# Six products in stage 1, one operand by an adding DMA, and VectorE's steps in another order

## The chip, the cores and the metric

The kernel runs on one core of a Trainium2 chip, in float32. The metric is the device time of one execution in microseconds, from the program's first to its last instruction with what lies around it; the time before is the median of three runs. The engines are TensorE (PE, with its weight loads as PEld), VectorE (DVE), ScalarE (ACT), GpSimd (POOL) and SyncE (SP), which here only issues DMAs.

## The reference

For each of 128 samples, `x` (64 channels, 1024 positions) goes through four convolutions whose weights are scaled by the sample's own style vector and normalised; the sum with `x` is the result.

```python
def _layer(x, style, w, b, mw, mb, typ):
    s = style @ mw.T + mb
    weight = SCALE * w * s[:, None, :, None]
    demod = lax.rsqrt(jnp.sum(weight * weight, axis=(2, 3)) + EPS)
    weight = weight * demod[:, :, None, None]
    if typ == 'same':
        out = jax.vmap(_conv_same)(x, weight) + b[None, :, None]
    elif typ == 'upsample':
        out = jax.vmap(_conv_up)(x, weight.transpose(0, 2, 1, 3)) + b[None, :, None]
        out = _blur(out, 2.0 * blur_k, (1, 1))
    elif typ == 'downsample':
        xb = _blur(x, blur_k, (2, 2))
        out = jax.vmap(_conv_down)(xb, weight) + b[None, :, None]
    return out
...
out = x
for i, typ in enumerate(('same', 'upsample', 'same', 'downsample')):
    out = _layer(out, style, weights[i], biases[i], mod_w[i], mod_b[i], typ)
return x + out
```

## The kernel before, in words

Nothing nonlinear lies between the four layers, so the kernel multiplies their kernels together, sample by sample, into one convolution of nine taps, and applies that to `x` once. The first and last three positions of each row are computed apart ("ends", the border work), in small pieces that are strewn over the turns.

Samples are handled in fours ("quads" q = 0 to 31), two in the upper and two in the lower 64 partitions; every matmul uses a 64 by 64 quarter of the array, four quarters side by side. A quad goes through these steps:

- Stage 1 multiplies layer 4's three scaled taps (`wd`, made by `scale3`) with layer 3's three taps into five taps `S`. It does not do the nine tap products: `w3x` and `w2n` also hold sums of neighbouring taps. `stage1_a` (line 461) runs five blocks of 64 columns, ScalarE copies four of them into `S` with a minus, and `stage1_b` (line 473) runs two blocks more; then two VectorE instructions (line 481, the "S step") make the last two taps out of PSUM and `S`, and GpSimd adds two slots (line 484).
- Stage 2 (`stage2`) multiplies `S` with the blurred taps `E` of layer 2 into seven taps `R`. Turns 5 to 27 do part of it a turn ahead: `share_sums` (line 499, VectorE), `share` (TensorE) and `share_copy` (ScalarE, line 529), which lays the shared part into the PSUM banks `psR` of the same pool that `psS` of stage 1 held. So the share copy waits for the S step, and the next turn's stage 2 waits for the share copy. Where a turn's stage 2 isn't shared, it writes those banks itself and waits for the S step directly.
- Stage 3 (`stage3_b`, `stage3_a`) makes the nine taps `Wf`, with GpSimd's `r_sums` (line 638) ahead of its last product; VectorE combines them into `H` (`combine_a`, `combine_b`).
- The convolution: `x` lies in three planes by position modulo 3. VectorE forms `G` in two steps, G2 (`in_g2`, one plane, line 712) and G01 (`in_g01`, two planes, line 712); out of `G` come T0 and T4 (`in04`, VectorE, line 790), T1 (`in1`) and T2 (`in2`, both GpSimd, lines 776 and 781); out of `x` comes T3 (`in3`, VectorE, line 761). Five products on TensorE, `conv0` to `conv4` (line 803), use T0 to T4; `sum1`, `sum2` and ScalarE's output copies (line 880) end it.

The main loop, `turn_of(q)`, works on four quads at once: outputs and products of q, products of n = q + 1, stages 2 and 3 and inputs of c = q + 2, stage 1 of s = q + 4. Each engine takes its instructions in the order in which this code is written. Turn 4 is the "entry" turn, with an order of its own; turns 0 to 3 are `early_turn`. A turn begins with `stage2(c)` on TensorE. One piece of side work stands in most turns on VectorE (table `SIDE`): turns 5 to 7 read small products out of the upper columns of the PSUM tile `Y` (`small_rest`) and turns 4 to 6 clear those columns (MEMSET, line 1524); turns 8 to 28 do border work. A VectorE access of `Y` waits until ScalarE has copied turn q's output plane out of it. Turns 10, 14, 15 and 19 also run border matmuls on TensorE just ahead of conv1.

Of the kernel before, what the change touches and what calls it, by code (L numbers as in the profile page):

```python
# [54 lines left out]
C = 64  # L55
K = 3
# [7 lines left out]
def kernel(  # L64
# [30 lines left out]
    gpool = ctx.enter_context(tc.tile_pool(name="gpool", bufs=1))  # L95
# [308 lines left out]
    w3x = const.tile([P, 5, C], F32, name="w3x")  # L404
    w2n = const.tile([P, 5, C], F32, name="w2n")
# [9 lines left out]
    def scale3(q, engs=(nc_a, nc_a)):  # L415
# [3 lines left out]
        for j in range(2):  # L419
            t = wd_pool.tile([P, 5, C], F32, tag="wd", name=f"wd{q}_{j}")  # L420
# [23 lines left out]
    EVEN = slice(0, K, 2)  # L444

    def stage1(q, pool=None, engs=(nc_a, nc_a), between=None):
# [3 lines left out]
        for k, (at, at1) in enumerate(((0, 3), (3, 1), (1, 4))):  # L450
            tap_matmul(ps, wd, at, 2, woi[2][:, k, :], EVEN, first=k == 0)
            tap_matmul(ps, wd, at1, 1, woi[2][:, k, :], slice(1, 2), last=k == K - 1)
# [3 lines left out]
        for r in range(2):  # L456
            scaled_copy(engs[r], flat(st[r][:, 1:6]), ps[r][:, : 5 * C], tB[:, q, r : r + 1])
# [3 lines left out]
    def stage1_a(q, ps=None):  # L461
# [3 lines left out]
        tap_matmul(ps, wd, 2, 2, w2n[:, 0, :], EVEN, first=True)  # L465
        tap_matmul(ps, wd, 3, 2, w2n[:, 2, :], EVEN)
        tap_matmul(ps, wd, 1, 1, w2n[:, 1, :], slice(1, 2))
        st, t = s_tiles(q)
        for r in range(2):
            scaled_copy(nc_a, flat(st[r][:, :4]), ps[r][:, C : 5 * C], tBn[:, q, r : r + 1])  # L470
        chain[q] = wd, ps, st, t

    def stage1_b(q):

        wd, ps, st, t = chain[q]
        tap_matmul(ps, wd, 2, 1, w2n[:, 3, :], slice(3, 4))
        tap_matmul(ps, wd, 4, 1, w2n[:, 4, :], slice(4, 5), last=True)
        for r in range(2):
            p1 = st[r][:, 0:1, :].to_broadcast([P, 2, C])
            sums = ps[r][:, 2 * C : 6 * C].rearrange("c (a b o) -> c a b o", a=2, b=2)[:, :, 0]  # L480
            nc_v.scalar_tensor_tensor(
                st[r][:, 4:6, :], sums, tB[:, q, r : r + 1], p1, op0=ALU.mult, op1=ALU.subtract
            )
        nc_g.tensor_add(t[:, :, 2], t[:, :, 2], t[:, :, 0])  # L484
# [14 lines left out]
    def share_sums(q):  # L499
        t = whole[q]  # L500
        nc_v.tensor_add(t[:, :, 6:8], t[:, :, 1:5:3], t[:, :, 2:6:3])
# [13 lines left out]
    def share(q, ps):  # L515
# [3 lines left out]
        chain_matmul(p12, E[:, 2], chain[q], slice(6, 7))  # L519
        chain_matmul(p34, E[:, 6], chain[q], slice(6, 7))  # L520
        chain_matmul(p34, E[:, 5], chain[q], slice(7, 8), True)
# [13 lines left out]
    def stage2_rest(q):  # L535
# [17 lines left out]
            (block(4), Ed[:, 5], slice(4, 5)),
            (block(5), E[:, 7], slice(5, 6)),
# [222 lines left out]

    def in2(q, eng):
# [13 lines left out]
    def product(q, m, ps, groups=range(K), alone=False):  # L792

        W, H_ = Wq[q]
        tag, i = SLOT[m]
        for g in groups:
            for s, rows in enumerate(HALF):
                for c, cols in enumerate(HALF):
                    if m in (0, 4):
                        w = W[rows, tap(m // 2, g), c, :]  # L800
                    else:
# [4 lines left out]
                        Ts[q, tag][rows, c, i, g : g + NB],  # L806
# [83 lines left out]

    raw = const.tile([P, 512], F32, name="raw")
# [97 lines left out]
    g1 = const.tile([P, 6, C], F32, name="g1")  # L989
# [732 lines left out]
```

## Time and profile before

| | |
|---|---|
| Runs | 474.98, 476.53 and 475.28 us; median 475.28 |
| Profiled execution, first to last instruction | 475.5 us (what lies around it is not shown) |
| TensorE busy, share of the span | 469.7 us, 99% |
| VectorE busy | 417.3 us, 88% |
| ScalarE busy | 312.0 us, 66% |
| GpSimd busy | 165.8 us, 35% |
| Mean granted TensorE clock | 0.998 |
| One turn without border matmuls (6 to 27) | 13.8 to 14.2 us |
| One turn with them | 15.5 to 16.6 us |
| Data moved by DMA | 70.71 MB, 149 GB/s |

A line of the timeline reads: start in us from the span's start, duration, engine, line of the kernel, operation, output <- inputs, shape, count. Where several instructions are drawn together, the duration is that of all of them. Matmuls are pipelined, so the start of the next group tells more than a group's end; a float32 matmul is two instructions. In the view of one line's instructions the three numbers are the shortest, median and longest duration in ns; in the list of DMA issues they are count, size and median time to landing.

### The profile page before, as it was taken

To read this page: it belongs to the slowest core of one execution; us is meant where nothing else is said; L and a number is where in the kernel's file an instruction comes from. 1 tells how busy PE (TensorE), PEld (TensorE's weight loads), DVE (VectorE), ACT (ScalarE), POOL (GpSimd) and SP (SyncE) were. 2 spreads that over 40 slices of the span, in tenths; PEclk is the share of its full clock that TensorE was granted. 3 is DMA by queue.
4 is the path that set the end of the run, shared out by engine and by line. 5 is a ranking of instruction groups with operands and counts; after the bars stand their busy time and mean duration, and the time that the engine had idled before them with its cause. 6 is when DMAs were issued, how large, how long until landed. Compare 5 with 4: busy or idle time off the path is not lost.

```text
span 475.5 us, 26771 instructions
## 1 busy us (share of the span) xinstructions
PE 469.7 (99%) x11932; PEld 349.5 (74%) x11932; DVE 417.3 (88%) x694; ACT 312.0 (66%) x711; POOL 165.8 (35%) x200
## 2 busy tenths in 40 slices
PE   9999999999999999999999999999999999999996
PEld 6987788777678876677776677766788787876653
DVE  3889998879989998899979899979998999999896
ACT  4565657577766676766667666667666777766464
POOL 3634033664444342233432233422333423243200
PEclk9999999999999999999999999999999999999999
DMA  5237456535445554345544454543555544455225
GB/s 176 71 115 224 150 151 180 152 113 177 139 145 166 166 166 136 123 150 169 163 150 126 130 168 152 178 124 121 152 164 169 164 145 147 148 152 161 80 91 193
DMA packets 52707, 70.71 MB, mean 149 GB/s; under 512 B 6000, under 2 KB 50672, under 8 KB 52592
## 3 DMA queue, kind: packets, MB, share of 16 engines
q1 hardware_dynamic: 52368, 68.78, 46.3%
q8 instruction: 93, 1.52, 1.4%
q10 hardware_dynamic: 224, 0.22, 0.1%
q14 instruction: 22, 0.18, 0.1%
HBM read 35.36 MB, written 33.62 MB: 145 GB/s over the span
## 4 chain that ended last, share of the span: by engine, by line
PE 99%; DVE 0%; ACT 0%; issue 0%
PE psA L803 47%; PE Y L803 12%; PE psR L506 9%; PE psW L621 7%; PE psA L621 7%; PE psS L428 6%; PE psR L589 5%; PE psA L506 2%; PE Y L1044 2%; PE Y L183 1%; PE Y L379 1%; PE psM L220 0%; PE psE L1044 0%; PE Y L255 0%; DVE o L882 0%; PE psM L255 0%
## 5 line engine op out<-in xcount | busy, mean ns | idle before, releaser
L803 PE MATMUL psA<-T,H 64*64 64x340 f32 x2304 | 185.9, 446 | 0.0
L803 PEld LDWEIGHTS psA<-T,H 64*64 64x64 f32 x2304 | 90.7, 133 | 46.9 <-issue 2.5
L712 DVE SCALAR_TENSOR_TENSOR G<-X 128x1376 f32<-128x1376 f32 (+2 forms) x65 | 78.0, 1206 | 0.2
L776 POOL TENSOR_TENSOR T<-G 128x684 f32<-128x684 f32 x28 | 46.3, 1652 | 73.7 <-DVE G L712 73.7
L484 POOL TENSOR_TENSOR S<-S 128x128 f32<-128x128 f32 x28 | 21.6, 772 | 139.7 <-ACT S L399 139.6
L399 ACT ACTIVATE R<-psR,tC 128x448 f32<-128x448 f32 x63 | 36.6, 631 | 43.6 <-PE psR L506 25.8
L803 PE MATMUL psA<-T,Wf 64*64 64x340 f32 x768 | 63.7, 446 | 0.0
L803 PE MATMUL Y<-T,Wf 64*64 64x340 f32 x768 | 62.4, 451 | 0.0
L712 DVE SCALAR_TENSOR_TENSOR Y<-m,psA 128x340 f32<-128x340 f32 x62 | 32.0, 516 | 28.2 <-PE psA L803 26.9
L399 ACT ACTIVATE psW<-psA 128x128 f32<-128x128 f32 x100 | 19.3, 268 | 49.1 <-PE psA L621 45.0
L790 DVE TENSOR_TENSOR T<-G 128x1368 f32<-128x1368 f32 (+1 forms) x33 | 50.8, 1541 | 0.0
L399 ACT ACTIVATE Wf<-psW,t 128x256 f32<-128x256 f32 (+2 forms) x76 | 32.7, 480 | 26.7 <-PE psW L621 26.4
L761 DVE TENSOR_TENSOR T<-X 128x684 f32<-128x684 f32 x32 | 47.7, 1492 | 0.0
L506 PE MATMUL psR<-S,E 64*64 64x64 f32 (+1 forms) x1472 | 46.8, 237 | 0.0
L781 POOL TENSOR_TENSOR T<-G 128x684 f32<-128x684 f32 x28 | 46.5, 1660 | 0.0
L428 PEld LDWEIGHTS psS<-wd,w2n 64*64 64x64 f32 x1120 | 35.1, 133 | 12.9 <-issue 0.3
L506 PEld LDWEIGHTS psR<-S,E 64*64 64x64 f32 x1472 | 39.5, 134 | 4.9 <-ACT psR L529 0.2
L803 PEld LDWEIGHTS Y<-T,Wf 64*64 64x64 f32 x768 | 30.3, 132 | 16.8
L803 PEld LDWEIGHTS psA<-T,Wf 64*64 64x64 f32 x768 | 29.8, 133 | 14.5
L880 ACT ACTIVATE o<-psA,tb,td 128x340 f32<-128x340 f32 x63 | 37.1, 648 | 5.0 <-PE psA L803 2.8
L880 ACT ACTIVATE o<-y,tb,td 128x340 f32<-128x340 f32 x62 | 38.5, 678 | 0.0
L880 ACT ACTIVATE o<-Y,tb,td 128x340 f32<-128x340 f32 x62 | 36.1, 639 | 2.8 <-PE Y L803 2.0
(180 smaller groups left out, 840.4 us busy)
## 6 DMA issues: line engine op xcount, KB each, us to landing
out<-o SPq DMA_DIRECT2D x191, 170.0 KB, 2.6
X<-in_x SPq DMA_DIRECT2D x150, 172.0 KB, 3.4
X<-in_x SPq DMA_DIRECT2D x14, 516.0 KB, 5.0
par<-in_params SPq DMA_DIRECT2D x3, 192.0 KB, 3.8
Xe<-in_x_ends SPq DMA_DIRECT2D x1, 512.0 KB, 4.5
out<-Oe SPq DMA_DIRECT2D x2, 96.0 KB, 2.1
out<-o ACTq DMA_DIRECT2D x1, 170.0 KB, 2.8
par<-in_params SPq DMA_DIRECT2D x1, 160.0 KB, 2.7
```

Source lines behind the costliest of these rows:

```text
L399: nc_a.activation(dst, src, AF.Copy, scale=f)
L428: nc.tensor.matmul(ps[r][cols, at * C : (at + n) * C], weight[rows], wd[c if r == 0 else 1 - c][rows, taps], start=first, stop=last, skip_ ...
L506: nc.tensor.matmul(dst[r][cols], weight[rows], st[c if r == 0 else 1 - c][rows, slots, :], start=False, stop=last, skip_group_check=True,)
L589: nc.tensor.matmul(ps[r][cols, lo * C : (lo + m) * C], E[rows, e + 2, :], src[rows, a, :], start=(n == 0), stop=(n == 8), skip_group_check ...
L621: nc.tensor.matmul(dst[r][cols], weight[rows], t[rows, c, slots, :], start=first, stop=last, skip_group_check=True,)
L712: nc_v.scalar_tensor_tensor(out, x, f, y, op0=ALU.mult, op1=op)
L761: nc_v.tensor_sub(t[:, pairs, 0, :NJ], plane(X, 3, pairs), plane(X, 1, pairs))
L776: eng.tensor_add(t[:, :, 0, :NJ], plane(g, 2), plane(g, 1))
L781: eng.tensor_sub(t[:, :, 1, :NJ], plane(g, 2), plane(g, 1))
L790: nc_v.tensor_sub(t[:, pairs, :, :NJ], both(a, PL), both(b, 1))
L803: nc.tensor.matmul(ps[s][cols, :NB], w, Ts[q, tag][rows, c, i, g : g + NB], start=(g == 0 and (m == 3 or alone)), stop=(g == K - 1), skip_ ...
L880: nc_a.activation(dst, src, AF.Identity, bias=add, scale=d3)
```

## The change

1. `stage1_a` and `stage1_b` make the five taps from six products of one block (64 columns) each: the three products of equal taps, and three of sums of two taps. `w3x`, `w2n` and `wd` get a sixth block, 0 + 2. `stage1_a` runs the three of equal taps with a minus, ScalarE writes them in four copies (two end taps, and the middle one twice), and GpSimd makes with an add and a subtract the slot that the middle tap needs. `stage1_b` runs the other three, and the S step has 192 columns for 128. The whole form, `stage1` (quads 0, 1, 2 and 6), keeps its nine blocks in three instructions for six. The order of the slots in `S` changes everywhere with it.
2. From the entry turn on, T1 is no longer a GpSimd add into a tile: a DMA issued from GpSimd behind `r_sums` adds one plane of `G` onto another in place, and conv1 reads `G` (25 DMAs). T2 is then made a turn earlier, before that DMA. `G` gets a second buffer; `g1` and `raw` move into other tensors' space.
3. On VectorE the side work stands ahead of G2, G01 directly behind G2 and so ahead of the S step, and T0/T4 of c stands behind `sum1`, ahead of T3, where in the turn after it stood T0/T4 of n. The second half of the `g1` step moves from behind T3 in turn 13 to turn 14's side work.

```diff
-    gpool = ctx.enter_context(tc.tile_pool(name="gpool", bufs=1))
+    gpool = ctx.enter_context(tc.tile_pool(name="gpool", bufs=2))
...
         for t, src in ((w3x, w3), (w2n, woi[2])):
-            nc_g.tensor_add(t[:, K:], src[:, : K - 1], src[:, 1:])
+            nc_g.tensor_add(t[:, K : K + 2], src[:, : K - 1], src[:, 1:])
+            nc_g.tensor_add(t[:, K + 2], src[:, 0], src[:, 2])
...
     def stage1_a(q, ps=None):
...
-        tap_matmul(ps, wd, 2, 2, w2n[:, 0, :], EVEN, first=True)
-        tap_matmul(ps, wd, 3, 2, w2n[:, 2, :], EVEN)
-        tap_matmul(ps, wd, 1, 1, w2n[:, 1, :], slice(1, 2))
+        for n, (i, at) in enumerate(((0, 1), (2, 3), (1, 4))):
+            tap_matmul(ps, wd, at, 1, w2n[:, i, :], slice(i, i + 1), first=n == 0)
         st, t = s_tiles(q)
         for r in range(2):
-            scaled_copy(nc_a, flat(st[r][:, :4]), ps[r][:, C : 5 * C], tBn[:, q, r : r + 1])
+            ends = ps[r][:, C : 5 * C].rearrange("c (a b o) -> c a b o", a=2, b=2)[:, :, 0]
+            scaled_copy(nc_a, st[r][:, 0:5:4, :], ends, tBn[:, q, r : r + 1])
+        for r in range(2):
+            middle = ps[r][:, None, 4 * C : 5 * C].to_broadcast([P, 2, C])
+            scaled_copy(nc_a, st[r][:, 5:8:2, :], middle, tBn[:, q, r : r + 1])
+        nc_g.tensor_add(t[:, :, 6], t[:, :, 0], t[:, :, 4])
+        nc_g.tensor_sub(t[:, :, 6], t[:, :, 6], t[:, :, 5])
...
     def stage1_b(q):
-        tap_matmul(ps, wd, 2, 1, w2n[:, 3, :], slice(3, 4))
-        tap_matmul(ps, wd, 4, 1, w2n[:, 4, :], slice(4, 5), last=True)
+        for n, (i, at) in enumerate(((3, 1), (4, 3), (5, 2))):
+            tap_matmul(ps, wd, at, 1, w2n[:, i, :], slice(i, i + 1), last=n == K - 1)
         for r in range(2):
-            p1 = st[r][:, 0:1, :].to_broadcast([P, 2, C])
-            sums = ps[r][:, 2 * C : 6 * C].rearrange("c (a b o) -> c a b o", a=2, b=2)[:, :, 0]
             nc_v.scalar_tensor_tensor(
-                st[r][:, 4:6, :], sums, tB[:, q, r : r + 1], p1, op0=ALU.mult, op1=ALU.subtract
+                flat(st[r][:, 1:4]),
+                ps[r][:, C : 4 * C],
+                tB[:, q, r : r + 1],
+                flat(st[r][:, 5:8]),
+                op0=ALU.mult,
+                op1=ALU.subtract,
             )
-        nc_g.tensor_add(t[:, :, 2], t[:, :, 2], t[:, :, 0])
...
+    def in1_dma(q):
+
+        g = Gs[q]
+        nc_g.dma_start(plane(g, 2), plane(g, 1), accum_op=ALU.add)
+        first_of[q] = g[:, :, :PL]
...
+        14: lambda: setup1(1),
...
-    LATE = {13: lambda: setup1(1)}
...
     def turn_of(q):
...
             r_sums(c, nc_g)
+            in1_dma(n)
             sum2(q)
-            in2(n, nc_g)
...
-        in04(n)
+        if entry:
+            in04(n)
         if sharing(q):
             share_sums(c + 1)
-        in_g2(c)
         side(SIDE, q)
         if q in SMALL:
             l, bs = SMALL[q]
             nc_v.memset(high(bs.stop - bs.start), 0.0)
+        in_g2(c)
+        in_g01(c)
         conv0(q, *((2,) if entry else range(K)))
...
         if s < NQ:
             stage1_b(s)
-        in_g01(c)
...
+        in2(c, nc_g)
         sum1(n)
+        in04(c)
         in3(c)
-        side(LATE, q)
-        if s == NQ:
-            in04(c)
-        in1(c, nc_g)
```

How VectorE's rows stand in the entry turn: before (the MEMSET clears Y's upper columns, L481 is the S step, L712 on G are G2 and G01).

```order
L790 TENSOR_TENSOR T_5_1826<-G_1507 128x4x342
L712 SCALAR_TENSOR_TENSOR G_1828<-X_105 128x2x342
L279 TENSOR_TENSOR nw<-dm,var 128x96
L280 SCALAR_TENSOR_TENSOR nw<-nw,dm 128x96
L281 SCALAR_TENSOR_TENSOR dm<-nw,dm 128x96
L1524 MEMSET Y 128x96
L481 SCALAR_TENSOR_TENSOR S_1818<-psS_0_1804,tB,S_1818 128x128
L481 SCALAR_TENSOR_TENSOR S_1818<-psS_1_1805,tB,S_1818 128x128
L712 SCALAR_TENSOR_TENSOR G_1828<-X_105 128x2x688
L712 SCALAR_TENSOR_TENSOR y_5_1872<-psA_1722,m_5_1802 128x680
L761 TENSOR_TENSOR T_6_1874<-X_105 128x2x342
```

In the changed kernel VectorE's rows of the same turn are these.

```order
L803 TENSOR_TENSOR T_5_1810<-G_1492 128x4x342
L279 TENSOR_TENSOR nw<-dm,var 128x96
L280 SCALAR_TENSOR_TENSOR nw<-nw,dm 128x96
L281 SCALAR_TENSOR_TENSOR dm<-nw,dm 128x96
L1539 MEMSET Y 128x96
L717 SCALAR_TENSOR_TENSOR G_1816<-X_105 128x2x342
L717 SCALAR_TENSOR_TENSOR G_1816<-X_105 128x2x688
L482 SCALAR_TENSOR_TENSOR S_1798<-psS_0_1784,tB,S_1798 128x192
L482 SCALAR_TENSOR_TENSOR S_1798<-psS_1_1785,tB,S_1798 128x192
L717 SCALAR_TENSOR_TENSOR y_5_1861<-psA_1702,m_5_1782 128x680
L803 TENSOR_TENSOR T_6_1863<-G_1816 128x4x342
L766 TENSOR_TENSOR T_6_1865<-X_105 128x2x342
```

G2 has moved from ahead of the MEMSET to behind it, G01 from behind the S step to ahead of it, and a second T0/T4 row has come in ahead of T3.

VectorE in turn 5, the first of the three whose side work reads Y (the rows on `cc`); before, from T0/T4 to T3:

```order
L790 TENSOR_TENSOR T_6_2062<-G_1828 128x4x342
L501 TENSOR_TENSOR S_1818<-S_1818 128x2x128
L712 SCALAR_TENSOR_TENSOR G_2065<-X_106 128x2x342
L980 TENSOR_TENSOR cc_149<-Y,a_142 128x96
L981 SCALAR_TENSOR_TENSOR cc_149<-b1s,cc_149 128x96
L1524 MEMSET Y 128x96
L481 SCALAR_TENSOR_TENSOR S_2057<-psS_0_2043,tB,S_2057 128x128
L481 SCALAR_TENSOR_TENSOR S_2057<-psS_1_2044,tB,S_2057 128x128
L712 SCALAR_TENSOR_TENSOR G_2065<-X_106 128x2x688
L712 SCALAR_TENSOR_TENSOR y_6_2132<-psA_1950,m_6_2060 128x680
L761 TENSOR_TENSOR T_7_2134<-X_106 128x2x342
```

VectorE in turn 5 of the changed kernel:

```order
L506 TENSOR_TENSOR S_1798<-S_1798 128x2x128
L995 TENSOR_TENSOR cc_148<-Y,a_141 128x96
L996 SCALAR_TENSOR_TENSOR cc_148<-b1s,cc_148 128x96
L1539 MEMSET Y 128x96
L717 SCALAR_TENSOR_TENSOR G_2059<-X_106 128x2x342
L717 SCALAR_TENSOR_TENSOR G_2059<-X_106 128x2x688
L482 SCALAR_TENSOR_TENSOR S_2046<-psS_0_2032,tB,S_2046 128x192
L482 SCALAR_TENSOR_TENSOR S_2046<-psS_1_2033,tB,S_2046 128x192
L717 SCALAR_TENSOR_TENSOR y_6_2128<-psA_1939,m_6_2053 128x680
L803 TENSOR_TENSOR T_7_2130<-G_2059 128x4x342
L766 TENSOR_TENSOR T_7_2132<-X_106 128x2x342
```

Ahead of the side work's read of Y only the share sums (on S) are left of what stood there; both G steps now stand between the side work and the S step, and T0/T4 between `sum1` (on y) and T3. The later turns are built the same way, with their own side work.

GpSimd in turn 12, from its R sums on (the row on S is the add of stage 1, the rows on T are T2 and T1); before:

```order
L638 TENSOR_TENSOR R_3858<-R_3858 128x2x128
L781 TENSOR_TENSOR T_13_3796<-G_3729 128x2x342
L484 TENSOR_TENSOR S_3991<-S_3991 128x2x64
L776 TENSOR_TENSOR T_14_4066<-G_3999 128x2x342
L638 TENSOR_TENSOR R_4128<-R_4128 128x2x128
```

GpSimd in turn 12 of the changed kernel:

```order
L643 TENSOR_TENSOR R_3896<-R_3896 128x2x128
L786 DMA G_3763<-G_3763 128x2x342
L472 TENSOR_TENSOR S_4029<-S_4029 128x2x64
L473 TENSOR_TENSOR S_4029<-S_4029 128x2x64
L794 TENSOR_TENSOR T_14_4105<-G_4040 128x2x342
```

The DMA stands where T2 stood, T2 (of the next quad) where T1 stood, and the one row on S has become two, of which the S step of the same turn needs the second.

More of the change, by code (lines that the diff above doesn't have):

```diff
@@ L449, in stage1 @@
         ps = unit(pool or ps_w, f"psS{q}")
[L450 to L452 removed]
+        for k in range(K):
+            tap_matmul(ps, wd, k, K, woi[2][:, k, :], slice(0, K), first=k == 0, last=k == K - 1)
         if between:
```

58 lines of the change are left out of this document (31 added, 27 removed).

## The prediction

> **What bounds the kernel now.** I read the page's busy times and chain first, then the busy times of single turns, then the waits of the weight loads.
>
> ```profile
> PE 469.7 (99%) x11932; PEld 349.5 (74%) x11932; DVE 417.3 (88%) x694; ACT 312.0 (66%) x711; POOL 165.8 (35%) x200
> PE 99%; DVE 0%; ACT 0%; issue 0%
> 201.25:215.10 13.85, 13.85 (x389) 9.80 (x385) 12.74 (x20) 9.80 (x24) 4.81 (x4) 1.00 0.49 155
> 287.67:301.51 13.84, 13.84 (x388) 9.78 (x382) 12.96 (x23) 9.47 (x24) 4.81 (x4) 1.00 0.49 156
> PEld psR L506 <- ACT psR L529: 0.2, 1, 0.2
> ```
>
> TensorE is the chain. In turns 12 and 18 (third and fourth line: stretch, length, then PE, PEld, DVE, ACT, POOL, clock) it is busy from end to end at clock 1.00, and VectorE has 1.1 and 0.9 us left. So a matmul saved is worth its full time, and anything that makes TensorE wait costs its full time. The last line says where it stands closest to a wait: stage 2 needs the share copy, and once its weights waited 0.2 us for it. The rest of the argument is about what runs ahead of that copy. Turn 12, TensorE first, then VectorE (start, duration, instruction):
>
> ```profile
> 210.53 0.73 PE L428 MATMUL psS<-wd,w2n 64*64 64x128 f32 x24
> 211.08 1.90 PE L803 MATMUL psA<-T,Wf 64*64 64x340 f32 x24
> 212.80 0.41 PE L428 MATMUL psS<-wd,w2n 64*64 64x64 f32 x16
> 213.03 0.53 PE L506 MATMUL psA<-S,E 64*64 64x64 f32 x24
> 215.10 0.40 PE L506 MATMUL psR<-S,E 64*64 64x128 f32 x8
> 207.90 0.56 DVE L712 SCALAR_TENSOR_TENSOR H<-H,Wf 128x384 f32<-128x384 f32 x1
> 210.03 1.58 DVE L790 TENSOR_TENSOR T<-G 128x1368 f32<-128x1368 f32 x1
> 211.53 0.42 DVE L501 TENSOR_TENSOR S<-S 128x256 f32<-128x256 f32 x1
> 211.86 0.87 DVE L712 SCALAR_TENSOR_TENSOR G<-X 128x684 f32<-128x684 f32 x1
> 212.64 0.81 DVE L1066 TENSOR_TENSOR Ye<-Ye,c 128x384 f32<-128x384 f32 x1
> 213.38 0.60 DVE L481 SCALAR_TENSOR_TENSOR S<-psS,tB,S 128x128 f32<-128x128 f32 x2
> 213.90 1.58 DVE L712 SCALAR_TENSOR_TENSOR G<-X 128x1376 f32<-128x1376 f32 x1
> 215.42 0.87 DVE L712 SCALAR_TENSOR_TENSOR y<-psA,m 128x680 f32<-128x680 f32 x1
> ```
>
> The S step (L481) leads the next stage 2 by 215.10 - 213.38 = 1.72 us. How small that lead may be is shown by turn 18, whose side work is the longest:
>
> ```profile
> 300.48 0.61 DVE L481 SCALAR_TENSOR_TENSOR S<-psS,tB,S 128x128 f32<-128x128 f32 x2
> 300.92 0.63 ACT L529 COPY psR<-psA 128x256 f32<-128x256 f32 x2 [0.62 <-DVE S L481]
> 301.51 0.42 PE L506 MATMUL psR<-S,E 64*64 64x128 f32 x6
> ```
>
> There the lead is 1.03 us, ScalarE's copy waited for the S step and ended as stage 2 began, and the turn is no longer than turn 12. So 1.03 us is enough and there is nothing below it.
>
> **The change part by part.**
>
> *Stage 1, TensorE.* 24 instructions (16 of 128 columns, 8 of 64) take 211.08 - 210.53 = 0.55 us, 16 of 64 take 0.23, so one of 64 is 14.4 ns and one of 128 is 27.2. Now 16 + 24 instructions cost 0.78 us; the change issues 48 of 64: 0.69. That is 0.09 us in each of 28 groups, 2.5 us. The four whole stages 1 lose 24 instructions each at equal columns; at the fixed part of 1.6 ns (14.4 less half of 25.6, twice the 12.8 per 64 columns) 0.15 us in all. Together **-2.7**, between -2.0 and -3.4, since a gain of 0.09 read from pipelined starts may be off by 0.025. [...]
>
> *The S step.* It has 192 columns for 128 in each of its two instructions. VectorE's 684 and 1376 columns (0.87 and 1.58) give 1.03 ns a column, so 0.07 each, 0.14 together: the lead needed becomes 1.17. Its first instruction now also reads the tile's slot that two GpSimd adds fill behind ScalarE's copies. GpSimd's one add of today (L484) has no reader near it. ScalarE's copies behind it become four of half the size; that they get done later by this is possible, and stands in the upper bound below.
>
> *What GpSimd's adds meet.* The next rows are GpSimd's add with VectorE idle, then in turn 7 beside a G01 step.
>
> ```profile
> 99.67 0.46 POOL L484 TENSOR_TENSOR S<-S 128x128 f32<-128x128 f32 x1 [0.58 <-ACT S L399]
> 142.56 1.58 DVE L712 SCALAR_TENSOR_TENSOR G<-X 128x1376 f32<-128x1376 f32 x1
> 142.83 1.62 POOL L484 TENSOR_TENSOR S<-S 128x128 f32<-128x128 f32 x1
> ```
>
> An add of 0.46 us took 1.62 and ended 0.37 after VectorE's G01 step gave way (142.56 + 1.52): it stood still until then. The other way round VectorE pays too: the 384-column side step of turn 12 took 0.81 beside the add, the H step of equal size 0.56, so 0.25. Now G01 (1.52 from start to start, 213.90 to 215.42) stands ahead of the S step where T0/T4 (1.50, 210.03 to 211.53) stood: even. The first add costs what the one add costs today. The second can only start when G01 lets go: 0.37, and I estimate 0.1 for the hand-over, 0.47 together; S is that much later in every turn. Bounds: 0, if the second add slips in ahead of G01, and 0.65, if both have to queue behind it.
>
> *Sixteen shared turns (8, 9, 11 to 13, 16 to 18, 20 to 27).* The first and the last of their S steps and stages 2:
>
> ```profile
> 156.06 0.60 DVE L481 SCALAR_TENSOR_TENSOR S<-psS,tB,S 128x128 f32<-128x128 f32 x2
> 157.72 0.48 PE L506 MATMUL psR<-S,E 64*64 64x128 f32 x7
> 427.69 0.60 DVE L481 SCALAR_TENSOR_TENSOR S<-psS,tB,S 128x128 f32<-128x128 f32 x2
> 429.36 0.40 PE L506 MATMUL psR<-S,E 64*64 64x128 f32 x8
> ```
>
> Their leads run from 1.03 to 1.76, 1.58 in the mean. Needed are 1.17 + 0.47 + 0.09 (stage 2 comes earlier by what stage 1 saves) = 1.73, so TensorE waits 0.15 a turn: **+2.4**. Bounds: +0.2 with no delay (only turn 18 is short) and +5.3 with 0.65. Turns 10, 14, 15 and 19 have border matmuls ahead of stage 2 and the room for it; turn 14 takes the moved half of the g1 step there for nothing.
>
> *The entry turn (4).* Here the clearing of Y's upper columns (MEMSET) is part of the side work.
>
> ```profile
> 99.47 1.17 ACT L880 ACTIVATE o<-Y,tb,td 128x340 f32<-128x340 f32 x2
> 100.74 0.14 DVE L1524 MEMSET Y<- 128x96 f32 x1 [2.39 <-ACT o L880]
> 100.79 0.53 DVE L481 SCALAR_TENSOR_TENSOR S<-psS,tB,S 128x128 f32<-128x128 f32 x2
> 101.21 2.71 PE L589 MATMUL psR<-S,E 64*64 64x192 f32 x70
> ```
>
> VectorE sits 2.39 us until ScalarE has read Y, clears it, does S, and stage 2, which writes the PSUM that S reads, starts 0.42 after S. Today G2 is done during that wait and G01 after S. In the new order both come between the MEMSET and S: 0.78 (211.86 to 212.64) + 1.52 = **+2.3** of standing TensorE, with nothing to cover it; I see no bound more than 0.2 from it.
>
> *Turns 5 to 7.* Their side work reads Y, so it too waits for ScalarE's output copies; today G2 and T0/T4 fill that time. Turn 5:
>
> ```profile
> 110.51 1.17 ACT L880 ACTIVATE o<-Y,tb,td 128x340 f32<-128x340 f32 x2
> 113.45 0.25 DVE L980 TENSOR_TENSOR cc<-Y,a 128x96 f32<-128x96 f32 x1
> 114.06 0.56 DVE L481 SCALAR_TENSOR_TENSOR S<-psS,tB,S 128x128 f32<-128x128 f32 x2
> 115.80 0.33 PE L506 MATMUL psR<-S,E 64*64 64x128 f32 x2
> ```
>
> Side work at 111.78 (110.51 + 1.17 and the 0.1 seen at the MEMSET), 0.61 of it (113.45 to 114.06), G2 0.78, G01 1.52, two adds held against them 0.25 each: S at 115.19. It should start at 115.80 - 0.09 - 1.17 = 114.54. TensorE waits 0.65; the two turns behind have the same pattern: **+1.9**, between +0.4 (adds cost nothing) and +2.4.
>
> *T1 by DMA.* GpSimd's add of 1.65 us goes, and with it what it did to T3, which runs right beside it; the DMA (350 KB in, 350 KB changed) is issued behind the R sums and must land before conv1, which comes behind the share matmuls of 213.03: some 7.6 us later.
>
> ```profile
> 204.72 0.73 POOL L638 TENSOR_TENSOR R<-R 128x256 f32<-128x256 f32 x1 [1.27 <-ACT R L399]
> L761 DVE TENSOR_TENSOR T<-X x32: 857/1764/1881, 15.9 to 455.1; 128x684 f32<-128x684 f32 x32
> X<-in_x SPq DMA_DIRECT2D x14, 516.0 KB, 5.0
> X<-in_x SPq DMA_DIRECT2D x150, 172.0 KB, 3.4
> ```
>
> No DMA from GpSimd and no adding one is in the trace. Nearest rows: 3.4 us for less, 5.0 for more; doubled for the second read, 10 us would be 2.4 late and cost 25 x 2.4 = 60 us. I take about 5, as near the bigger load: hidden, **0**. T3 falls from 1.76 to about 0.86, but VectorE then only waits longer for conv2, so that is 0 too. In return T0/T4's 1.50 us now stands between conv1 and conv2. T3's 0.9 and the 1.1 us that VectorE has left in turn 12 cover it; without the gain on T3, 0.4 us a turn would be lost. SP's loads behind T3 start that much later and have most of a turn.
>
> Sum on the profiled execution's span of 475.5: -2.7 + 2.3 + 1.9 + 2.4 = +3.9. The median of the runs is 475.28, 0.2 below that span, and what lies around the span is not shown; I put the difference on the median: **479.2 us**.
>
> **The rivals.**
>
> *The adds do not hold S up* (they slip in ahead of G01, or VectorE is late enough anyway). For it: GpSimd is busy 35% and its copies come early. Against it: the 1.62 us add. Then -2.7 + 2.3 + 0.4 + 0.2 = +0.2, 475.5: no change. It decides if the delay of S stays under 0.2 us. With the full 3.4 us for stage 1 and the entry turn as forecast it ends at 474.8, and only past that on the fast side.
>
> *T1 lands late.* For it: loads and stores hold the queues at 0.49 already. Against it: 7.6 us of room. Every half microsecond late is 25 x 0.5 = 12.5 us: 491.7.
>
> [...]
>
> **How the numbers follow.** About 0.3% (1.4 us) is what a measurement of this kernel can tell from no change. The forecast case has 0.65: between +1.2 and +7.5, of which 0.04 is within 0.3%. The adds not in the way 0.22: 0.06 faster, 0.13 same, 0.03 slower. T1 late 0.10 and descriptors held 0.03, slower. Faster 0.06, same 0.17, slower 0.77. The range, 474.9 to 484.0, takes in most of the second case and the upper bounds of the forecast (-2.0 + 2.4 + 2.4 + 5.3 = +8.1, 483.4); it leaves out T1 late and the fastest corner.
>
> **What would show it.** Stage 1's group near 0.69 us a turn; a TensorE gap of about 2.3 us before stage 2 at 101 us, put down to S; gaps of 0.1 to 0.7 in shared turns, longest in 5 to 7 and 18, released by ScalarE's share copy, which itself waits for S, and S for GpSimd; GpSimd's second add ending about 0.4 behind G01. Wrong it would be if the adds end before G01 starts, if conv1 waits for the DMA, or if the adding DMA itself takes GpSimd so long that the adds start late.

## The result: 2.9% slower

The changed kernel takes 489.3 us (four runs, 487.75 to 491.81), the kernel before 475.62: a ratio of 1.0288, 95% interval 1.026 to 1.0315. Forecast were 479.2 us and a range up to 484.0: the direction held, the size did not. The profiled execution spans 488.8 us. Two lines of its page (busy times, the chain that ended last) and one of its DMA issues:

```profile
PE 478.3 (98%) x12060; PEld 355.9 (73%) x12060; DVE 402.6 (82%) x694; ACT 324.5 (66%) x767; POOL 189.5 (39%) x230
PE 91%; DVE 4%; issue 2%; POOL 1%; ACT 1%; DVEq 0%; ACTq 0%
G<-G POOLq DMA_DIRECT2D x25, 342.0 KB, 6.0
```

TensorE was 99% of the chain; VectorE, GpSimd, ScalarE and "issue" now hold 8%. To place the loss, both timelines are cut at the starts of stage 2, counted from the first of them (10.40 and 10.31 us), since what lies ahead of it differs from execution to execution (8.3 to 10.6 us in the kernels below):

| Stretch | before | changed | difference |
|---|---|---|---|
| turns 0 to 3 | 78.19 | 78.50 | +0.31 |
| entry turn 4 and turn 5 | 27.21 | 32.05 | +4.84 |
| turns 6 and 7 | 28.01 | 29.00 | +0.99 |
| turns 10, 14, 15, 19 | 63.36 | 63.73 | +0.37 |
| sixteen shared turns | 222.19 | 228.39 | +6.20 |
| turn 28 and the end | 46.11 | 46.77 | +0.66 |

**A shared turn.** Two turns of the changed kernel side by side (stretch, length, busy PE, PEld, DVE, ACT, POOL, clock): turn 11, the only shared turn that loses nothing, and turn 12.

```profile
195.25:209.00 13.75, 13.75 (x396) 9.57 (x390) 11.77 (x19) 8.32 (x22) 4.98 (x5) 1.00 0.65 165
209.00:223.03 14.03, 14.03 (x397) 10.37 (x394) 11.77 (x19) 10.28 (x26) 5.64 (x6) 1.00 0.66 179
```

Turn 11's 13.75 us, for 13.84 before, is what stage 1 saves. Turn 12 is 0.28 longer than that. Its timeline, VectorE's G2 with G01 and its S step, GpSimd's adds, the share copy and the next stage 2:

```profile
218.84 2.36 DVE L717 SCALAR_TENSOR_TENSOR G<-X 128x684 f32<-128x684 f32 x2
222.09 0.74 DVE L482 SCALAR_TENSOR_TENSOR S<-psS,tB,S 128x192 f32<-128x192 f32 x2 [0.89 <-POOL S L473]
219.82 1.69 POOL L472 TENSOR_TENSOR S<-S 128x128 f32<-128x128 f32 x1 [5.28 <-ACT S L399]
221.59 0.46 POOL L473 TENSOR_TENSOR S<-S 128x128 f32<-128x128 f32 x1
222.59 0.63 ACT L534 COPY psR<-psA 128x256 f32<-128x256 f32 x2 [0.60 <-DVE S L482]
223.03 0.41 PE L511 MATMUL psR<-S,E 64*64 64x128 f32 x4
```

G01 ends at 221.20. The first add stands until then and ends at 221.51, the second follows whole, and S starts 0.89 us behind G01. Stage 2's first weight load waits 0.39 us for the copy, whose second half ends 0.19 us after stage 2 has begun. So it goes in nearly every turn (us in all, times, longest wait):

```profile
DVE S L482 <- POOL S L473: 17.8, 23, 0.9
ACT psR L534 <- DVE S L482: 16.8, 22, 1.1
PEld psR L511 <- ACT psR L534: 8.2, 17, 0.8
```

Not all 23 waits of S are alike: 18 are 0.89 us long, those of turns 5, 6, 7, 10 and 18 are 0.35. In turns 5 to 7 the first add starts beside G2, ahead of G01, so it is the second that is held. Turn 5, the two adds and S:

```profile
117.23 0.92 POOL L472 TENSOR_TENSOR S<-S 128x128 f32<-128x128 f32 x1 [3.71 <-ACT S L399]
118.23 1.69 POOL L473 TENSOR_TENSOR S<-S 128x128 f32<-128x128 f32 x1
119.95 0.74 DVE L482 SCALAR_TENSOR_TENSOR S<-psS,tB,S 128x192 f32<-128x192 f32 x2 [0.35 <-POOL S L473]
```

**The entry turn** and what follows it, first the timeline, then TensorE's clock (the last column but two) in short stretches behind it:

```profile
101.26 0.14 DVE L1539 MEMSET Y<- 128x96 f32 x1 [3.30 <-ACT o L897]
101.31 2.35 DVE L717 SCALAR_TENSOR_TENSOR G<-X 128x684 f32<-128x684 f32 x2
103.58 0.74 DVE L482 SCALAR_TENSOR_TENSOR S<-psS,tB,S 128x192 f32<-128x192 f32 x2
104.04 4.55 PE L594 MATMUL psR<-S,E 64*64 64x192 f32 x70 [2.11 <-DVE S L482]
```

```profile
102.00:104.00 2.00, 0.00 (x0) 0.00 (x0) 2.00 (x4) 2.00 (x5) 0.20 (x1) 1.00 0.89 313
104.60:105.20 0.60, 0.60 (x16) 0.60 (x12) 0.60 (x2) 0.00 (x0) 0.60 (x1) 0.50 1.04 136
105.20:106.00 0.80, 0.80 (x18) 0.80 (x14) 0.80 (x1) 0.00 (x0) 0.24 (x1) 0.50 0.92 203
107.00:107.60 0.60, 0.60 (x16) 0.60 (x13) 0.60 (x1) 0.00 (x0) 0.00 (x0) 0.50 0.04 14
108.20:108.80 0.60, 0.60 (x20) 0.52 (x14) 0.00 (x0) 0.29 (x1) 0.00 (x0) 1.00 0.32 57
```

TensorE waits 2.11 us for S, as forecast. Then the granted clock is 0.50 from 104.5 to 107.9 us: stage 2 takes 4.55 us for 2.71, and the pause is paid nearly twice.

**Issue.** Weight loads stand still for 0.3 to 0.65 us in eight places between 100 and 460 us, 3.7 us in all, and the profile names no engine and no DMA for it ("issue"); before there are three places, 1.4 us. Matmuls already under way cover part of it: their own gaps put down to issue come to 1.3 us there, before to 0.2.

### The profile page after: what moved, and what is told of

Its sections match the earlier page's. It is cut to its first block, busy times and chain, and to the rows that moved or that the text cites. A ratio compares the mean times of both kernels' runs of the same rounds, so it can differ in the third digit from the quotient of the medians.

```text
span 488.8 us, 27140 instructions
## 1 busy us (share of the span) xinstructions
PE 478.3 (98%) x12060; PEld 355.9 (73%) x12060; DVE 402.6 (82%) x694; ACT 324.5 (66%) x767; POOL 189.5 (39%) x230
## 4 chain that ended last, share of the span: by engine, by line
PE 91%; DVE 4%; issue 2%; POOL 1%; ACT 1%; DVEq 0%; ACTq 0%
PE psA L820 41%; PE Y L820 11%; PE psR L511 11%; PE psA L626 7%; PE psW L626 7%; PE psR L594 5%; PE psS L429 4%; PE Y L1060 2%; PE psA L511 2%; POOL S L473 1%; DVE H L717 1%; DVE G L717 1%; ACT S L399 1%; PE Y L183 1%; PE Y L379 1%
## 5 line engine op out<-in xcount | busy, mean ns | idle before, releaser
L820 PE MATMUL psA<-T,H 64*64 64x340 f32 x1704 | 140.8, 447 | 0.4 <-DVE y L717 0.4
L820 PEld LDWEIGHTS psA<-T,H 64*64 64x64 f32 x1704 | 75.4, 133 | 28.7 <-issue 2.3
L472 POOL TENSOR_TENSOR S<-S 128x128 f32<-128x128 f32 x28 | 38.2, 1364 | 145.1 <-ACT S L399 145.1
L511 PEld LDWEIGHTS psR<-S,E 64*64 64x64 f32 x1472 | 46.7, 134 | 12.7 <-ACT psR L534 8.2
L511 PE MATMUL psR<-S,E 64*64 64x64 f32 (+1 forms) x1472 | 54.5, 241 | 1.4 <-issue 0.7
L794 POOL TENSOR_TENSOR T<-G 128x684 f32<-128x684 f32 x28 | 46.6, 1665 | 9.2 <-PE psA L820 6.0
L643 POOL TENSOR_TENSOR R<-R 128x256 f32<-128x256 f32 x24 | 17.5, 728 | 83.5 <-ACT R L399 64.1
L820 PE MATMUL psA<-G,H 64*64 64x340 f32 x600 | 48.0, 446 | 0.0
L429 PEld LDWEIGHTS psS<-wd,w2n 64*64 64x64 f32 x1344 | 32.8, 134 | 13.3 <-issue 0.5
L626 PEld LDWEIGHTS psA<-R,w0s 64*64 64x64 f32 x1000 | 35.6, 133 | 3.4 <-ACT R L399 0.4
```

The lines of the kernel that those rows point to most:

```text
L429: nc.tensor.matmul(ps[r][cols, at * C : (at + n) * C], weight[rows], wd[c if r == 0 else 1 - c][rows, taps], start=first, stop=last, skip_ ...
L472: nc_g.tensor_add(t[:, :, 6], t[:, :, 0], t[:, :, 4])
L511: nc.tensor.matmul(dst[r][cols], weight[rows], st[c if r == 0 else 1 - c][rows, slots, :], start=False, stop=last, skip_group_check=True,)
L626: nc.tensor.matmul(dst[r][cols], weight[rows], t[rows, c, slots, :], start=first, stop=last, skip_group_check=True,)
L643: eng.tensor_add(t[:, :, 7:9], t[:, :, 2:6:3], t[:, :, 3:7:3])
L794: eng.tensor_sub(t[:, :, 1, :NJ], plane(g, 2), plane(g, 1))
```

## Experiments

### Parts alone and in pairs

The change has three parts: the six products, the adding DMA (with T2 made a turn earlier), and VectorE's order (G2 behind the side work, G01 ahead of S). T0/T4 stand ahead of T3 wherever the DMA or the new order does. First each part alone, and the DMA with the six products. `six_only`: the lines of stage 1 and of the slots as changed, and `g1` and `raw` in other tensors' space; all else as before. `order_only`, against the kernel before:

```diff
-        in04(n)
+        if entry:
+            in04(n)
...
-        in_g2(c)
         side(SIDE, q)
...
+        in_g2(c)
+        in_g01(c)
         conv0(q, *((2,) if entry else range(K)))
...
             stage1_b(s)
-        in_g01(c)
...
         sum1(n)
+        in04(c)
         in3(c)
```

`six_dma`, against the changed kernel:

```diff
+        in_g2(c)
         side(SIDE, q)
...
-        in_g2(c)
-        in_g01(c)
...
             stage1_b(s)
+        in_g01(c)
```

`dma_only` is `six_dma` with stage 1 as before.

> The kernel before with the six products alone: VectorE's old order, T1 on GpSimd, no DMA from GpSimd. Theory A (the S step is held by GpSimd's two adds only where VectorE's G01 stands ahead of it): the adds run beside G2 and T0/T4, S comes at most some tenths later and keeps more than 1.2 us ahead of stage 2, so the saving shows: 475.6 - 2.7 = 472.9 us (472.5 to 474.0). Rival B (the adding DMA costs the time): the same 472.9, since there is no DMA. Rival C (the six products cost the time wherever they stand, because the adds make S late in any order): 477 us or more.

> The kernel before with VectorE's new order alone (side work ahead of G2, G01 ahead of the S step, T0/T4 ahead of T3); seven blocks and one late add, T1 on GpSimd. Theory A: nothing on GpSimd holds S up, so S follows G01 at once and shared turns lose nothing; the entry turn loses 2.3 us and turns 5 to 7 some 0.5 each: 475.6 + 2.3 + 1.5 = 479.4 us (478 to 481). Rival B: the same. Rival C': the order alone costs it all: 486 us or more, with S late in every shared turn. A fourth outcome, T3 late for conv2 because T1 runs beside it, would give 25 x 0.4 = 10 us on top of A.

> The changed kernel without the six products and with G2, side work, S step and G01 in the old order: the adding DMA and T0/T4 ahead of T3 are left. Theory A: no change but a few late instruction fetches, 475.6 us (475 to 477.5). Rival B (the adding DMA costs the time, by its traffic and by what TensorE's instructions wait for): 479 to 488 us, with gaps on TensorE put down to issue in many turns.

> The changed kernel with one thing undone: G2 stands again ahead of the side work and G01 behind the S step. Theory A: the waits of S for GpSimd's second add fall from 0.9 us to under 0.2, the gap of the entry turn (4.3 us over two turns) goes, and 12 to 16 us of the loss with them: 473 to 476 us. Rival B: 479 us or more, since the DMA stays. Rival C: 480 us or more, since the six products and their adds stay.

Measured were 478.21, 479.18, 493.04 and 494.45 us, with 476.57 for the kernel before beside them. The order alone costs 2.8 us by its ratio, for 3.8 expected, and not where it was expected: the entry turn loses 2.3 us as forecast, turn 5 loses 1.9 (the clock falls there too: 0.59 in the mean of 102.2 to 104.5 us, 0.62 from 104.5 to 106.5), and turns 6 and 7 lose nothing, since no add holds S up. The six products alone did not gain, which by the number is rival C; but in the trace S waits for an add in five turns only, 0.35 us each. Against the kernel before 2.0 us lie in one turn (14, below), 0.8 in turn 9, with a gap of 1.0 us put down to issue, and 0.7 ahead of turn 6.

The first theory fell, and rival B seemed right: with the DMA and the old order the time is the worst of all, above B's own 488 us. But the waits say otherwise. `dma_only` from G01 to conv4 in turn 12, VectorE, then GpSimd, then TensorE, and the wait over the whole run:

```profile
203.93 1.58 DVE L712 SCALAR_TENSOR_TENSOR G<-X 128x1376 f32<-128x1376 f32 x1
206.29 2.49 DVE L798 TENSOR_TENSOR T<-G 128x1368 f32<-128x1368 f32 x1
208.70 1.40 DVE L761 TENSOR_TENSOR T<-X 128x684 f32<-128x684 f32 x1
205.66 1.68 POOL L789 TENSOR_TENSOR T<-G 128x684 f32<-128x684 f32 x1 [2.91 <-DVE G L712]
211.13 1.95 PE L815 MATMUL Y<-T,Wf 64*64 64x340 f32 x24 [0.79 <-DVE Y L712]
```

```profile
PEld Y L815 <- DVE Y L712: 17.2, 20, 1.5
```

T2 on GpSimd now waits for G01. Where G01 is late, T2 runs beside T0/T4, which take 2.49 us for 1.58; T3 runs beside the R sums and takes 1.40 for 0.86. So sum2 is late, and conv4 waits for it: a turn takes 14.77 us for 13.85. That T2's place costs this, and not the DMA's traffic, is theory A2 of the next runs.

> The changed kernel with the old stage 1 (seven blocks, one late add): the DMA and VectorE's new order are left. By the run with the DMA and the old order, 0.92 us a turn went to conv4, which waits for sum2, because T2 on GpSimd follows a late G01 and runs beside T0/T4. Theory A2 (that collision, and not the DMA's traffic, was the price there): with G01 ahead of S, T2 is over before T0/T4 starts, S waits for no add, and only the entry turn and turn 5 lose (4.2 us, as in the run of the order alone): 476.6 + 4.2 = 480.8 us (479.5 to 482.5). Rival B (the DMA's traffic and late instructions cost the time in any order): 486 us or more.

> The changed kernel without the DMA (T1 and T2 on GpSimd as before, one buffer for G): six products and VectorE's new order. Theory A2: S follows GpSimd's second add 0.9 us behind G01 in every turn, as in the changed kernel, so TensorE loses 0.3 to 0.5 us a turn, and the entry turn and turn 5 lose 4.8: 476.4 + 10 = 486.5 us (484.5 to 488), with hardly any TensorE gaps put down to issue. Rival B (the DMA's traffic is the main cost): 480 us or less.

`no_six` is the changed kernel with stage 1 as before. `six_order`, against the changed kernel:

```diff
-            in1_dma(n)
             sum2(q)
+            in2(n, nc_g)
...
-        in2(c, nc_g)
         sum1(n)
         in04(c)
         in3(c)
+        in1(c, nc_g)
...
```

They took 482.13 and 486.04 us, both near A2's figure. All eight combinations, as ratio to the kernel before with its 95% interval:

| | no DMA | with the DMA |
|---|---|---|
| seven blocks, old order | 1 | 1.0355 (1.0330 to 1.0381) |
| six products, old order | 1.0031 (1.0014 to 1.0049) | 1.0381 (1.0357 to 1.0406) |
| seven blocks, new order | 1.0059 (1.0040 to 1.0079) | 1.0106 (1.0081 to 1.0130) |
| six products, new order | 1.0230 (1.0204 to 1.0255) | 1.0288 (1.0260 to 1.0315) |

The parts do not add up. With the DMA, and so with T2 a turn earlier, the new order saves 2.5% (seven blocks); with the six products and no DMA it loses 2%: G01 early gets T2 away from T0/T4, and holds the adds. `six_order` has the changed kernel's wait without any DMA:

```profile
DVE S L482 <- POOL S L473: 17.1, 23, 0.9
```

Its sixteen shared turns lose 3.9 us against before, 5.3 with the saving of stage 1 counted.

### T2 back in its place

`dma_t2_back`, against `dma_only`:

```diff
             r_sums(c, nc_g)
+            in2(n, nc_g)
             in1_dma(n)
...
-        in2(c, nc_g)
...
```

> The run of the DMA with the old order, and T2 back where it stood before, on GpSimd behind the R sums, the DMA behind it. Theory A2 (conv4 was late because T2 ran beside T0/T4): T0/T4 takes 1.6 us for 2.5, conv4's waits of 0.8 to 1.5 us go, and the time falls from 493.0 to 477 to 479 us; if the DMA, issued 1.7 us later, then lands behind conv1's start, TensorE waits for it there by name and the time stands between. Rival B (the DMA delays T0/T4's result or TensorE by its traffic): 488 us or more, with T0/T4 still at 2.5 us.

476.75 us, ratio 1.0023 (1.0008 to 1.0038). In turn 12, VectorE and GpSimd:

```profile
202.56 1.58 DVE L798 TENSOR_TENSOR T<-G 128x1368 f32<-128x1368 f32 x1
205.60 1.65 POOL L789 TENSOR_TENSOR T<-G 128x684 f32<-128x684 f32 x1
```

Out of T2's way T0/T4 take 1.58 us, conv4 waits no more, and 16 us are back. The edit also moves the DMA, but `no_six`, with the DMA early and G01 early, had no such loss either: A2 is shown. The DMA, issued 2.0 us later in the turn (6.1 us after its start for 4.1), still lands in time.

### The adds and the entry turn

`no_adds` and `entry_old`, each against the changed kernel:

```diff
-            middle = ps[r][:, None, 4 * C : 5 * C].to_broadcast([P, 2, C])
-            scaled_copy(nc_a, st[r][:, 5:8:2, :], middle, tBn[:, q, r : r + 1])
-        nc_g.tensor_add(t[:, :, 6], t[:, :, 0], t[:, :, 4])
-        nc_g.tensor_sub(t[:, :, 6], t[:, :, 6], t[:, :, 5])
+            middle = ps[r][:, None, 4 * C : 5 * C].to_broadcast([P, 3, C])
+            scaled_copy(nc_a, st[r][:, 5:8, :], middle, tBn[:, q, r : r + 1])
```

```diff
         if entry:
             in04(n)
+            in_g2(c)
...
-        in_g2(c)
-        in_g01(c)
+        if not entry:
+            in_g2(c)
+            in_g01(c)
...
             stage1_b(s)
+        if entry:
+            in_g01(c)
```

> The changed kernel without GpSimd's add and subtract in stage 1 (they are left out: slot 6 gets a third copy of the middle tap, so the taps are not the reference's). Theory A2: S follows G01 at once, 0.9 us earlier in each turn; the 0.3 to 0.4 us that TensorE loses in shared turns go, and 0.9 in the entry turn: 481 us (479.5 to 483). Rival B: the DMA still costs what it costs, 486 us or more.

> The changed kernel with the old order in the entry turn alone (G2 ahead of the MEMSET, G01 behind the S step). The entry turn and turn 5 together hold 4.8 us of the loss in the changed kernel. Theory A2: that goes, but T2 of the entry turn now follows a late G01, runs beside T0/T4, and conv4 of turn 5 waits some 1.5 us, as in the run with the DMA and the old order: 489.3 - 4.8 + 1.5 = 486.0 us (485 to 487.5). If the collision is not what delayed conv4 there, 484.5.

`no_adds`, which leaves GpSimd's add and subtract out: 484.44 us (ratio 1.0180, 1.0148 to 1.0212), 1.4 above the expected range. Turns of 13.76 us come back (12, 13, 16, 17, 22, 23), and S waits for no add. The 0.9 us expected in the entry turn did not come (15.38 us for 15.23): S waits for no add there in the changed kernel either. And this execution has gaps put down to issue of 5.7 us, 2 more than the changed kernel: the price of the adds shows in those turns, and a second cost stays.

`entry_old`: 487.43 us (1.0228, 1.0208 to 1.0247), within the expected range. The entry turn falls from 15.23 to 12.96 us, and conv4 of turn 5 waits 1.5 us for sum2, as A2 said. Without the pause the clock stays up in the stretch where the changed kernel had 0.50:

```profile
99.83:102.40 2.57, 2.57 (x74) 2.44 (x72) 2.57 (x4) 2.57 (x5) 0.65 (x1) 1.00 0.91 316
```

### Issue gaps: bytes of the DMA

`six_t2_back` joins the six products to `dma_t2_back`, both causes taken away. `six_small_dma` and `six_no_dma`, against it (T1 is mostly or wholly not formed in them):

```diff
-        nc_g.dma_start(plane(g, 2), plane(g, 1), accum_op=ALU.add)
+        nc_g.dma_start(plane(g, 2)[:, :, :8], plane(g, 1)[:, :, :8], accum_op=ALU.add)
```

```diff
-        nc_g.dma_start(plane(g, 2), plane(g, 1), accum_op=ALU.add)
```

> The changed kernel with G2 and G01 in their old places and T2 back behind the R sums, the DMA behind it: both causes found so far taken away, the six products kept. In the same form with seven blocks VectorE stood 1.6 us idle ahead of the S step, so GpSimd's two adds end in time. Theory A2: S waits for no add, conv4 for no sum2, the turns run at the saving of 0.09 us each, less 0.6 us in the early and entry turns: 476.8 - 1.6 = 475.2 us (474 to 476.5), equal to the kernel before or 0.5 us below it. Rival B (six products and DMA together bring TensorE gaps put down to issue, some 3 us in the changed kernel): 478 us.

> The run with six products, the DMA, G in its old order and T2 back, with the adding DMA cut to 8 of 342 columns of each row (so T1 is mostly not added): as many DMAs, descriptors and instructions, a fortieth of the bytes. That run had TensorE gaps put down to issue of 4.0 us between 100 and 460 us and times from 475.1 to 480.8. Theory I1 (the bytes of the DMA delay TensorE's instructions): gaps fall to 0.5 to 2 us and the time to 474.5 us (473.5 to 475.5). Theory I2 (GpSimd's DMA itself, its descriptors or its issue): they stay at 3 us or more, 477 us. Theory I3 (the six products alone, by how fast TensorE uses up its instructions): they stay here and without any DMA.

> The same kernel with the adding DMA left out altogether (T1 is not formed; conv1 reads the plane as it is). Theories I1 and I2: gaps of 0.5 to 2 us, 474.5 us (473.5 to 475.5), since nothing else holds S or conv4 up and the six products' 0.09 us a turn show. Theory I3: gaps of 3 us or more and 477 us, as with the DMA.

477.41 us (475.13 to 480.81, ratio 1.0023, 1.0005 to 1.0041), then 476.29 (1.0009, 0.9992 to 1.0026) and 475.87 (0.9996, 0.9979 to 1.0013). In `six_t2_back` S waits for no add and conv4 for no sum; what is left is issue. Its largest such wait, then that of the small DMA:

```profile
PEld psA L820 <- issue: 4.7, 12, 0.9
```

```profile
PEld psA L820 <- issue: 2.6, 7, 0.9
```

The gaps of 0.3 us and more fall from 4.0 us to 1.5 and 2.1. But each is one execution, and the one of `six_t2_back` was the slowest of its twelve (480.81 us), so part of the fall may be that. More weight has the whole set: the five kernels with the six products and the full DMA have gaps of 3.0 to 5.7 us, all others 0 to 2.4. By the gaps theory I1 fits (it takes the DMA's bytes, and the six products with them), and rival B has a share. By the times it isn't shown: beside the kernel before they fall by 0.14% and 0.27% (0.7 and 1.3 us), with intervals that overlap, and 476.29 and 475.87 us lie above the 473.5 to 475.5 that I1 gave. What TensorE lacks there stays open. The page of the changed kernel, then that of the kernel before, shows instructions coming by DMA:

```profile
q8 instruction: 94, 1.54, 1.4%
q8 instruction: 93, 1.52, 1.4%
```

That is 16.4 KB a packet, and one packet more than before; no run here shows such a packet and a gap together.

### A version that gains

Four kernels without the DMA look for stage 1's 2.5 us. `six_late14` and `six_g1`, against `six_only`; `six_t1_dve`, against `six_no_dma`; and the core of `six_best`, against `six_t1_dve` (for the quads named, with copies, S step and one add as in the kernel before):

```diff
-    LATE = {13: lambda: setup1(1)}
+        14: lambda: setup1(1),
...
```

```diff
-        10: setup0,
+        10: lambda: (setup0(), setup1(0), setup1(1)),
-        13: lambda: setup1(0),
-    LATE = {13: lambda: setup1(1)}
...
```

```diff
         if entry:
             in04(n)
+        else:
+            in1(n, nc_v)
...
```

```diff
+        if q in (3, 4, 5, 7, 8):
+            tap_matmul(ps, wd, 2, 2, w2n[:, 0, :], even, first=True)
+            tap_matmul(ps, wd, 3, 2, w2n[:, 2, :], even)
+            tap_matmul(ps, wd, 1, 1, w2n[:, 1, :], slice(1, 2))
...
```

> The run of the six products alone, with the second half of the g1 step moved from behind T3 in turn 13 to turn 14's side work. In that run it took 2.63 us for 0.74 (its first instruction beside GpSimd's T2) and conv4 of turn 14 waited 1.9 us for sum2. Expected: 478.2 - 2.1 = 476.1 us (475 to 477). If g1 is slow because it now lies in another tensor's space, turn 14's S step is late instead and nothing is gained: 478 us.

> The six products alone, with both halves of the g1 step in turn 10's side work, where border matmuls give room. In the run with the second half in turn 14, TensorE waited 0.8 us there for g1's border matmuls. Expected: that 0.8 us goes and nothing else moves: 475.3 us (474.5 to 476.2), 1 us below the kernel before. If turn 10 or 11 becomes late instead (S or conv4 behind 1.5 us more of side work), 476.5.

> The run without the DMA (six products, G in its old order, T2 behind the R sums, T0/T4 behind sum1), with T1 formed on VectorE where T0/T4 stood before, so that everything is computed again. T1 takes 0.86 us of the 1.6 us that VectorE stands idle there. If VectorE has that room: turns of 13.76 us and 475.9 us, as in the run without T1, equal to the kernel before. If S becomes late by it: 477 us or more.

> The same, with the old seven blocks and their one late add for the quads of the early turns and the entry turn (3, 4, 5, 7 and 8), where the six products lose 0.9 us before turn 6 (0.3 in turns 0 to 3, 0.3 in the entry turn, 0.3 in turn 5) because S waits there for ScalarE's copies and GpSimd's adds. Expected: 475.9 - 0.9 = 475.0 us, 0.2% below the kernel before; if that loss has another cause, 475.9.

What the first of them undoes, in turn 14 of `six_only`: the g1 step ran into GpSimd's T2 and took 2.63 us for 0.74, sum2 was late and conv4 waited.

```profile
231.42 2.63 DVE L1020 SCALAR_TENSOR_TENSOR nw<-par,nw 128x192 f32<-128x192 f32 x2
232.08 1.75 POOL L786 TENSOR_TENSOR T<-G 128x684 f32<-128x684 f32 x1
235.07 1.95 PE L808 MATMUL Y<-T,Wf 64*64 64x340 f32 x24 [1.90 <-DVE Y L717]
```

`six_late14`: 476.09 us, as expected, 1.0004 of before (0.9987 to 1.0022). `six_g1` did not give the 475.3 us expected: 477.50 (1.0045); turn 14 gained 0.55 us, but turns 11 and 13 lost 0.5 each. `six_t1_dve`: 476.30 us, 1.0006 (0.9991 to 1.0022), with thirteen of the sixteen shared turns at 13.75 to 13.78 us. `six_best`: 475.17 us, **0.9976 (0.9960 to 0.9993)**, the only one whose interval lies below the kernel before, and near the 475.0 expected. Not so its parts: in the profile the early turns give 0.66 us for the 0.3 expected, the entry turn nothing (12.97 us for 12.95) and turn 5 0.1. Its turn 12, VectorE (T1, G2, S) and GpSimd's second add:

```profile
209.54 0.87 DVE L808 TENSOR_TENSOR T<-G 128x684 f32<-128x684 f32 x1
210.66 0.86 DVE L744 SCALAR_TENSOR_TENSOR G<-X 128x684 f32<-128x684 f32 x1
212.76 0.74 DVE L509 SCALAR_TENSOR_TENSOR S<-psS,tB,S 128x192 f32<-128x192 f32 x2 [0.51 <-PE psS L430]
211.92 0.65 POOL L487 TENSOR_TENSOR S<-S 128x128 f32<-128x128 f32 x1
```

T0/T4 behind sum1 leave VectorE time ahead of S; the adds end at 212.57, and S waits for stage 1 itself. So the six products can pay, with the adds clear of G01, T2 clear of T0/T4, no DMA, and seven blocks where S has no room. It is 0.24%, in the best of four versions, and no run has this arrangement with seven blocks throughout; that the gain is the six products' is argued from the turns: undisturbed shared turns take 13.75 us in the kernels with six products, 13.84 in those with seven blocks.

## Why the prediction was wrong, point by point

- *Stage 1, TensorE* (-2.7): right where nothing waits (13.75 for 13.84 us a turn, here and in `six_best`). The -0.15 for the whole stages is lost in a loss that was not forecast: turns 0 to 3 are 0.3 us longer, turn 3 by 0.45 (15.86 for 15.41), where seven blocks with the DMA had 15.40.
- *What GpSimd's adds meet*: the mechanism was right, the size not. "The second can only start when G01 lets go: 0.37, and I estimate 0.1 for the hand-over, 0.47 together" is the case in which the first add comes ahead of G01; where the trace has that, in turns 5 to 7, S waits 0.35 us. In nearly all shared turns the first add is the one that is held, and the second's own 0.46 lies behind it: 0.89 was measured. The bound of 0.65 for this case was short of it.
- *The lead that S needs*: 1.17 us was too much. "So 1.03 us is enough and there is nothing below it" failed: in `six_order` stage 2 starts 0.91 to 1.01 us behind S in all sixteen shared turns. With both sizes as measured the forecast's own sum would be 0.92 + 0.89 + 0.09 - 1.58 = 0.32 us a turn, 5.1 in all (an estimate). The term of the *sixteen shared turns*, +2.4, measured 5.3 (`six_order`). That this is the upper bound to the digit is luck: two wrong sizes cancel in it.
- *The entry turn* (+2.3): the wait was 2.11 us, as forecast. "I see no bound more than 0.2 from it" failed: the halved clock adds 1.7.
- *Turns 5 to 7* (+1.9): turn 5 lost 0.5 behind stage 2, turns 6 and 7 together 1.0; with the saving of 0.09 each 1.8. Right, and by the mechanism: G2 and G01 take 2.61 us for the 2.36 of turn 12, and S then waits 0.35 for the held add, 0.6 together for the 0.5 that was counted.
- *T1 by DMA* (0): right that it is hidden (about 5 us to landing was assumed, 6.0 measured; conv1 does not wait), and that T0/T4 is covered; the last holds only because T2, made early, was over by then. The forecast says nothing of T2's new place on GpSimd, directly behind G01, which costs 0.92 us a turn as soon as G01 is late. Missed as well were the issue gaps, 2.3 us more than before; from `six_order` to the changed kernel the ratio grows by 0.58%, 2.8 us.
- *The rivals*: the adds did hold S up. T1 landed in time here; in `no_six` and `no_adds` one weight load waited 0.3 us for it. The 0.03 on descriptors held is a term that no run shows: GpSimd's DMA instruction took 1.18 to 1.37 us in the changed kernel, in 24 of 25 cases with VectorE busy for 90% or more of that time. So none of these happened.
- *The sum*: spread over the stretches of the table, the forecast is -0.5, 2.8, 1.1, -0.4, 1.0 and 0, measured were 0.3, 4.8, 1.0, 0.4, 6.2 and 0.7. Of the 9.4 us missed 5.2 lie in the shared turns (2.9 of it the adds, by `six_order`, and 2.3 what the DMA added to that kernel; the gaps there grew by 2.7), 2.1 in the entry turn and turn 5 (1.7 of it the clock) and 2.1 in the small stretches. There weight loads wait 1.0 us for S in turns 0 to 3 and 0.5 for the share copy at the end; the rest is not traced to a cause.

## What to carry to other kernels

When two short operations stand behind a step that holds their engine still, the reader behind them pays the wait and then the whole of the last one (0.89 us here, 0.46 of it the last add), so count the chain to its end. Ask of each moved operation what it will now run beside: the same G01 step cost 2.0% where it came early (beside the adds) and 2.5% where it came late (T2 then ran beside T0/T4), and no part alone told of the pair. A pause of TensorE can cost more than its length: 2.1 us cost 3.8 here.

## What the runs showed of the hardware

- After a pause of 2.11 us TensorE's granted clock fell to 0.50 in the changed kernel, from 104.5 to 107.9 us. Behind pauses of 2.07 to 2.14 us at the same place it fell in four other kernels: to 0.50 in `no_six` (106 to 108 us) and `six_order` (104.2 to 106.4), to a mean of 0.59 and 0.62 in `order_only` (102.2 to 104.5 and 104.5 to 106.5) and of 0.62 and 0.60 in `no_adds` (102.65 to 105 and 105 to 107). With 0.50 for as long as it was low, the means of these and the next stretches give 3.3 to 3.4 us each time, starting 0.4 to 1.5 us behind the pause's end (an estimate). After 1.90 us (turn 14 of `six_only`) and 1.26 us (turn 5 of `entry_old`) it stayed at 1.00.
- Steps of VectorE and GpSimd took longer where they overlapped. T0/T4 took 2.49 us for 1.58 where T2 had started on GpSimd 0.63 us ahead of it (turn 12 of `dma_only`), GpSimd's add 1.69 for 0.46 where G01 had started ahead of it (turn 12 of the changed kernel): in both the step that started later is the long one, while T2 took 1.68 us there (1.65 in `dma_t2_back`) and G2 with G01 2.36. In turn 5, beside two adds of 0.92 and 1.69 us, G2 with G01 took 2.61. The g1 step took 2.63 us for 0.74 beside the R sums and T2 (turn 14 of `six_only`).
- A DMA that adds 342 KB in place landed after 5.9 us (median of 25, `dma_only`) when issued right behind the R sums, after 4.8 (`dma_t2_back`) when issued 2.0 us later in the turn; in the changed kernel after 6.0.
